# Values times output projection in four 64x64 parts of the array

## The chip, the cores and the metric

The kernel runs on one core of one Trainium2 chip. The metric is the device time of one execution in microseconds (us). A core has five engines that work at the same time, each on its own queue of instructions: TensorE (PE in the profile; PEld is its weight load) multiplies matrices into PSUM, VectorE (DVE) and ScalarE (ACT) copy and compute, GpSimd (POOL) sets constants and starts indirect transfers, and SyncE (SP) starts the other transfers. They wait for one another by semaphores. PSUM has eight banks here; a product writes to one of them and a copy by ACT or DVE takes it out.

## The reference

The reference is one layer of cross attention with a mixture of experts behind it, all in fp32. Queries come from x (4 batches of 1,024 rows of 256), keys and values from a context of 77 rows per batch, with 16 heads of 64:

```python
x = x + xattn(ctx, layernorm(x), fside, fside, ln1_w, ln1_b, ln2_w, ln2_b, Wq, Wkv, Wout)
x = x + ffn(layernorm(x), Wr, Wg, Wu, Wd)      # 9 experts, the two best of each row

# in xattn: queries from x, keys k and values v from the context
qk = einsum('bihd,bjhd->bhij', q, k) * DIM_HEAD ** -0.5
attn = softmax(qk, axis=-1)
out = einsum('bhij,bjhd->bihd', attn, v)       # 16 heads side by side: 1024 columns
return out.reshape(b, -1, INNER) @ Wout
```

What matters here is the last two lines. For a head h, attn_h @ v_h @ Wout_h can be computed as attn_h @ (v_h @ Wout_h). The product v_h @ Wout_h doesn't depend on the queries: it has 77 rows (one for each key) and 256 columns, and is computed once for each batch and head.

## The kernel before, in words

The work has a setup, an attention stage and an expert stage.

The setup loads the context and the weights, normalises the context, and forms two tables for each batch. `g` folds keys with Wq, so that scores are z @ g for a normalised tile z of x. `u` is values times output projection, with nine more columns behind the 256, the router's logits of the same rows (`DE` = 265 columns in all, filled into `wo_sb` by `turn_logits`). `g_half` and `u_half` each hold two batches.

The attention stage takes 32 tiles of 128 rows of x. In tile i the loop issues the scores of tile i in three banks (`scores`: products, then a maximum on DVE), their exponentials on ACT (`exponentials`), then turns the weights of tile i-1 (`weights_turn` on TensorE, `weights_copy` on ACT) and multiplies them with `u` (`values`). `attention_weights` sums and divides on DVE. The expert stage follows with the lists of rows that the router made.

All is issued by hand: `tc.manual_schedule()` leaves each engine's instructions in the order in which the program writes them. An engine works through its queue in this order.

**How u is laid out before.** A key table of 77 rows is split into `JA` = 64 first keys and `JR` = 13 others. Two heads (2n and 2n+1) share one chunk of 128 rows: chunk n of `u` holds the first keys of head 2n in its upper half and those of head 2n+1 in its lower half. That makes `NP` = 8 chunks. The other keys of all 16 heads lie in `NR` = 2 more chunks, padded: a pair of heads has 26 rows in a strip of `W` = 32. So `values` is a sum over `KC` = 10 products.

**How u is computed before.** `context_values(n)` multiplies the normalised context with the value weights of heads 2n and 2n+1; head 2n comes out in partitions 0 to 63 of the bank (64 features), head 2n+1 in 64 to 127. The copies place them block by block into `vbd` (line 589), a table of zeros in which head 2n has the upper left 64x64 block and head 2n+1 the lower right one. `first_keys(b, n)` multiplies this block-diagonal 128x128 table with the 128 rows of Wout of both heads (line 739), and one copy puts the bank into `u`. `other_keys(n)` does it for the other keys of all four batches at once (line 745), and four copies of 26 rows put them into their strips, one for each batch. `evict` gives a copy to DVE for an odd number and to ACT for an even one.

In the order of the queues, five value products come first, with the turn of Wout and the logits between them. The statistics of the first queries follow (`query_stats` to `query_scale`), then eight rounds n: value products while there are any left, four `first_keys`, and one `other_keys` in the middle. In the last rounds the first two tiles of queries and the scores of tile 0 stand between them. The bank of a product comes from `bank_tile`, which uses all eight banks in turn, or from `mm_tile`, which uses five of them once the scores need the other three.

SP's queue holds, in this part, two loads of x, 16 small transfers that put the keys' offsets into the last row of `g` (line 676), and a third load of x.

Of the kernel before, what the change touches and what calls it, by code (L numbers as in the profile page):

```python
# [8 lines left out]
F32 = mybir.dt.float32  # L9
I32 = mybir.dt.int32  # L10
U32 = mybir.dt.uint32
AF = mybir.ActivationFunctionType
ALU = mybir.AluOpType
AX = mybir.AxisListType

P = 128
# [5 lines left out]
def kernel(  # L22
# [18 lines left out]
    nc = tc.nc  # L41

    B, N, D = x.shape
    J = ctx_in.shape[1]
# [16 lines left out]
    NR = 2  # L61
    HR = H // NR
    KC = NP + NR
    W = 32
    NA = KC * P
    DE = D + E
    HB = TB // J
    banks = [(h, min(HB, H - h)) for h in range(0, H, HB)]
    assert banks[-1][1] * J + E <= TB
    assert FT == 64 and DH == 64 and C == 2 and 2 * JR <= W and NP * W == NR * P  # L70
    ATT_SCALE = DH**-0.5


# [48 lines left out]
    def mm_tile(name):  # L122
        return ps_mm.tile([P, TB], F32, tag="mm", name=name)
# [3 lines left out]
    def bank_tile(name):  # L127

        turn_of[0] = (turn_of[0] + 1) % 8
        if turn_of[0] < 5:  # L130
            return mm_tile(name)
        k = turn_of[0] - 5
        return ps_sc.tile([P, TB], F32, tag=f"sc{k}", name=name)

    def evict(k, dst, src):

        if k % 2:
            nc.vector.tensor_copy(dst, src)
        else:
            nc.scalar.copy(dst, src)  # L140
# [65 lines left out]
    def query_stats(g, s):  # L206
        if g not in zstats:
            zstats[g] = stat.tile([P, NS, 6], F32, tag="bnq", name=f"bn_q{g}", bufs=2)
        return nc.vector.bn_stats(zstats[g][:, s, :], xg[g][:, s, :])
# [81 lines left out]
    def attention_weights(i):  # L291

        ex = exs.pop(i)
        sm = stat.tile([P, H], F32, tag="sm", name=f"sm{i}")
        nc.vector.tensor_reduce(sm, ex, AX.X, ALU.add)  # L295
        rs = stat.tile([P, H], F32, tag="rs", name=f"rs{i}")
        nc.vector.reciprocal(rs, sm)
        an = ans[i] = an_of[i % 2]
        nc.vector.tensor_tensor(  # L299
            an[:, : H * JA].rearrange("p (h j) -> p h j", h=H), ex[:, :, 0:JA],  # L300
            rs.unsqueeze(2).to_broadcast([P, H, JA]), ALU.mult,
        )
        nc.vector.tensor_tensor(
            an[:, H * JA :].rearrange("p (n w) -> p n w", w=W)[:, :, : 2 * JR].rearrange(
                "p n (t j) -> p n t j", t=2
            ),
            ex[:, :, JA:J].rearrange("p (n t) j -> p n t j", t=2),
            rs.rearrange("p (n t) -> p n t", t=2).unsqueeze(3).to_broadcast([P, NP, 2, JR]),
            ALU.mult,
        )  # L310

    TURNS = [(k, min(4, KC - k)) for k in range(0, KC, 4)]
# [40 lines left out]
        nc.vector.bn_stats(fstats[g][:, s, :], xg[g][:, s, :])  # L353


    with tc.tile_pool(name="vside", bufs=1) as vside, ExitStack() as kvs:
        kside = kvs.enter_context(tc.tile_pool(name="kside", bufs=1))

        crows = kside.tile([2, D], F32, name="crows")
# [146 lines left out]
        nc.vector.memset(cfold_all, 0.0)  # L506
        cfold = cfold_all[:, :, : 2 * B].rearrange("p n (t b) -> p n t b", t=2)

        TURN = NP - NP // 2
        kT = kside.tile([P, NP, B * J], F32, name="kT")  # L510
        kTs = kside.tile([P, NP, B * J], F32, name="kTs")
# [74 lines left out]
                wc, wr_sb, mean.unsqueeze(1).to_broadcast([P, C, E]), ALU.subtract  # L586
            )

        vbd = vside.tile([P, NP, B, P], F32, name="vbd")
        first = nc.gpsimd.memset(vbd, 0.0)  # L590
        tc.add_manual_dep(
            first.ins, normed.ins.name,
            mybir.DependencyInfo(mybir.DependencyClass.Sync, mybir.DependencyReason.DATA),
            reason="VectorE's work in front of TensorE's first products comes first",
        )
        vrem = vside.tile([P, NP, B, W], F32, name="vrem")
        nc.gpsimd.memset(vrem, 0.0)
        for i in range(2):
            nc.gpsimd.memset(u_half[i][:, :, NP:, :], 0.0)

# [39 lines left out]
        for n in range(NP):  # L640
            if n == 2:
                turn_offsets()
            if n == NP // 2:
                router_weights()
            if n == NP - 2:
                numbers()
            for c in range(C):
                for t in range(2):
                    half = slice(64 * t, 64 * t + 64)
                    pg = bank_tile(f"pgk{n}_{c}_{t}")  # L650
                    nc.tensor.matmul(
                        pg[:, : B * J], wqT[half, n, c * P : (c + 1) * P], kTs[half, n, :],
                        start=True, stop=True,
                    )
                    h = 2 * n + t
                    src = pg[:, : B * J].rearrange("p (b j) -> p b j", b=B)
                    at = slice(h * J, (h + 1) * J)
                    evict(t, g_half[0][:, :, c, at], src[:, :BH])
                    evict(t, g_half[1][:, :, c, at], src[:, BH:])
# [12 lines left out]
        for b in range(B):  # L672
            nc.vector.tensor_copy(g_sb[b][:, :, HJ:], wz)
            for t in range(2):
                for k in range(NP // QT):
                    nc.sync.dma_start(
                        out=g_sb[b][P - 1 : P, C - 1, :HJ].rearrange(
                            "p (k q t j) -> p k q t j", q=QT, t=2, j=J
                        )[:, k, :, t, :],
                        in_=brow.rearrange("(q r) k m -> q r k m", q=QT)[  # L680
                            :, t * B + b, k, b * J : (b + 1) * J
                        ],
                    )
# [25 lines left out]
        def turn_logits():  # L709
            pt = bank_tile("pwlt")  # L710
            for q in range(QB):
                nc.tensor.transpose(
                    pt[:, q * 2 * WC : (q + 1) * 2 * WC], wl[:, q * P : (q + 1) * P],
                    ident[: 2 * WC, : 2 * WC],
                )
            nc.vector.tensor_copy(
                wo_sb[:, :, D:].rearrange("p (i q) e -> p i q e", i=2),
                pt[:, : QB * 2 * WC].rearrange("p (q i e) -> p i q e", q=QB, i=2)[:, :, :, :E],
            )

        def context_values(n):
            pv = bank_tile(f"pv{n}")
            for c in range(C):
                nc.tensor.matmul(
                    pv[:, : B * J], wv_sb[:, c, n * P : (n + 1) * P], cT[:, c, :],
                    start=(c == 0), stop=(c == C - 1),
                )
            for t in range(2):
                half = slice(64 * t, 64 * t + 64)
                src = pv[half, : B * J].rearrange("p (b j) -> p b j", b=B)  # L730
                evict(n, vbd[half, n, :, t * JA : (t + 1) * JA], src[:, :, 0:JA])
                evict(n, vrem[half, n, :, t * JR : (t + 1) * JR], src[:, :, JA:J])

        def key_tile(name, n):
            return bank_tile(name) if n < NP - 1 else mm_tile(name)

        def first_keys(b, n):
            pu = key_tile(f"pu{b}_{n}", n)
            nc.tensor.matmul(pu[:, :DE], vbd[:, n, b, :], wo_sb[:, n, :], start=True, stop=True)
            evict(n + b, u_sb[b][:, n, :], pu[:, :DE])  # L740

        def other_keys(n):

            pu = key_tile(f"pur{n}", n)
            nc.tensor.matmul(
                pu[:, :DE], vrem[:, n].rearrange("p b w -> p (b w)"), wo_sb[:, n, :],
                start=True, stop=True,
            )
            r, q = divmod(n, P // W)
            for b in range(B):  # L750
                evict(
                    n, u_sb[b][q * W : q * W + 2 * JR, NP + r, :],
                    pu[b * W : b * W + 2 * JR, :DE],
                )

        EARLY_V = 5
        QB = TB // P
        for n in range(EARLY_V):
            if n < 2:
                for c in range(C):  # L760
                    turn_wo(n * QB, c)
            elif n == 3:
                wo_logits()
            context_values(n)
        turn_logits()
        for q in range(NS):
            query_stats(0, q)
        query_variance(0)
        query_root(0)
        query_scale(0)  # L770
        for n in range(NP):
            last = n == NP - 1
            if n + EARLY_V < NP:
                context_values(n + EARLY_V)
            if n >= NP - 2:
                query(n - NP + 2)
            for b in range(B):
                if last and b == 2:
                    query_turn(1)
                first_keys(b, n)  # L780
                if b == 1:
                    other_keys(n)
                if last and b < len(banks):
                    scores(0, b)
                    exponentials(0, b)
            if n == 0:

                nc.scalar.activation(junk, eps_t, AF.Exp)
            if n == NP - 2:
                query_turn(0)  # L790
    sent = []

    def after(i, others, reason):
# [587 lines left out]
    for i in range(N_SUB + 1):  # L1381
# [4 lines left out]
        if now_on:  # L1386
# [9 lines left out]
            if i:  # L1396
                scores(i, 2)
        if i:
            weights_turn(i - 1)
            weights_copy(i - 1, 0)  # L1400
            weights_copy(i - 1, 1)
        if now_on and i:
            exponentials(i, 1)
        if 0 < i < N_SUB - 1:
# [149 lines left out]
```

## Time and profile before

| | |
|---|---|
| time, median of 3 runs | 927.01 us (924.75 to 927.33) |
| the profiled execution | 924.82 us |
| its span in the profile | 922.8 us |
| granted TensorE clock, mean | 0.997 |
| TensorE busy | 906.7 us, 98% of the span |
| first keys, line 739 | 64 records, 16.6 us busy |
| other keys, line 745 | 16 records, 4.9 us busy |
| copies of other keys on DVE / on ACT | 6.9 us / 5.9 us busy, 16 each |
| transfers into g, line 676 | 16, issued from 33.93 to 42.99 us |
| first scores of tile 1 begin | 69.75 us |
| first values of tile 0 begin | 76.39 us |

Times in the profile are microseconds from the start of the span. A group line names source line, engine, operation, the tiles written and read, shapes, the count, and after the bar the busy time in us and the mean length of one in ns; behind the second bar stands the idle time before them, with what ended it. An fp32 product shows as two records of MATMUL and two of LDWEIGHTS. `128*64` ahead of a matmul's shape means that 128 rows and 64 columns of the array are in use. The length of a matmul record holds its way through the array, so the pace of a stream is read from the distance of starts. A line of the windows gives a stretch, its length, the busy time of PE, PEld, DVE, ACT and POOL, the granted clock, the busy share of the transfer engines and GB/s.

### The profile page before, as it was taken

The numbers are of one execution on the slowest core, as the hardware profiler recorded it, in microseconds if no ns is written. First come the engines' busy times: TensorE is split into PE (matmuls) and PEld (weight loads), VectorE is DVE, ScalarE is ACT, GpSimd is POOL, SyncE is SP. The second block draws the span as 40 slices with busy tenths as digits, with TensorE's granted clock in tenths as the row PEclk, the third lists the DMA queues.
The fourth block names the chain that finished last, engine by engine and source line by source line (L and its number), as shares of the span: only waits on it lengthen the run. The fifth ranks groups of instructions, "written<-read, shape, count | busy, mean of one in ns | idle before, by whom it ended". The sixth has DMA issues, their size and how long they took to land. (4 is left out here: it accounts for less than half of the span.)

```text
span 922.8 us, 13371 instructions
## 1 busy us (share of the span) xinstructions
PE 906.7 (98%) x4210; PEld 703.5 (76%) x4210; DVE 450.0 (49%) x1330; ACT 341.7 (37%) x1075; POOL 318.2 (34%) x329
## 2 busy tenths in 40 slices
PE   8999999999999999999999999999999999999996
PEld 6676777777777777788888777777777777778885
DVE  5776678888788887763722222222222222222221
ACT  4666575565646566551211122222222222111210
POOL 5000000321504242146454445435435435444432
PEclk9999999999999999999999999999999999999998
DMA  6200010503102710456779779779779777779822
GB/s 216 70 0 1 24 46 25 46 24 46 51 30 59 229 30 24 117 153 172 179 209 299 217 207 307 212 211 313 218 205 310 219 208 227 218 220 312 226 35 23
DMA packets 109125, 137.02 MB, mean 148 GB/s; under 512 B 24247, under 2 KB 79039, under 8 KB 109056
## 3 DMA queue, kind: packets, MB, share of 16 engines
q1 hardware_dynamic: 91498, 118.78, 42.0%
q0 software_dynamic: 17344, 17.26, 10.5%
q8 instruction: 34, 0.56, 0.3%
q14 instruction: 35, 0.29, 0.1%
q10 hardware_dynamic: 214, 0.13, 0.0%
HBM read 119.48 MB, written 18.33 MB: 149 GB/s over the span
## 5 line engine op out<-in xcount | busy, mean ns | idle before, releaser
L1193 PE MATMUL pg<-xT,wgu 128*128 128x256 f32 x1144 | 251.7, 379 | 0.4 <-PEq L1510 0.4
L1193 PEld LDWEIGHTS pg<-xT,wgu 128*128 128x128 f32 x1144 | 215.9, 190 | 29.3 <-issue 0.8
L1267 PE MATMUL po<-wd,hid 128*128 128x256 f32 (+1 forms) x804 | 180.5, 379 | 0.0
L1267 PEld LDWEIGHTS po<-wd,hid 128*128 128x128 f32 (+1 forms) x804 | 147.2, 187 | 21.3 <-issue 0.7
L275 ACT ACTIVATE ex<-psc,mx 128x77 f32<-128x77 f32 x512 | 124.2, 361 | 101.8 <-DVE mx L265 96.7
L1302 POOL DMA_INDIRECT out_dram<-co,ids x63 | 100.7, 1599 | 170.4 <-DVE co L1270 136.4
L918 POOL DMA_INDIRECT list_d<-r_entry,r_pli x64 | 67.2, 1050 | 256.2 <-DVE r_pli L916 124.9
L338 PE MATMUL po<-u,aT 128*128 128x265 f32 x640 | 151.7, 391 | 0.9 <-ACT aT L327 0.8
L261 PE MATMUL psc<-g,zT 128*128 128x462 f32 (+1 forms) x384 | 139.1, 511 | 1.2 <-ACT zT L250 1.2
L338 PEld LDWEIGHTS po<-u,aT 128*128 128x128 f32 x640 | 118.7, 189 | 23.7 <-ACT aT L327 1.9
L1200 DVE TENSOR_TENSOR hid<-pg,sl 128x256 f32<-128x256 f32 x130 | 55.1, 424 | 160.0 <-ACT sl L1199 159.7
L1199 ACT ACTIVATE sl<-pg 128x256 f32<-128x256 f32 x130 | 49.8, 384 | 218.3 <-PE pg L1193 211.9
L261 PEld LDWEIGHTS psc<-g,zT 128*128 128x128 f32 x384 | 72.5, 189 | 59.2 <-issue 49.4
L1270 DVE TENSOR_SCALAR co<-po,ids 128x256 f32<-128x256 f32 x67 | 32.4, 484 | 136.2 <-PE po L1267 136.1
L1151 POOL DMA_INDIRECT yin<-y_d,ids x67 | 70.4, 1051 | 24.7 <-issue 14.7
L265 DVE TENSOR_REDUCE mx<-psc 128x6 f32<-128x462 f32 (+1 forms) x96 | 55.7, 581 | 18.1 <-PE psc L261 15.1
L295 DVE TENSOR_REDUCE sm<-ex 128x16 f32<-128x1232 f32 x32 | 45.9, 1435 | 37.1 <-ACT ex L275 37.1
L327 ACT COPY aT<-pa 128x512 f32<-128x512 f32 (+1 forms) x96 | 49.4, 552 | 26.7 <-PE pa L319 26.7
L319 PEld LDWEIGHTS pa<-ident,an 128*128 128x128 f32 x320 | 36.9, 141 | 7.7 <-PE po L338 1.4
L319 PE MATMUL pa<-ident,an 128*128 128x128 f32 x320 | 40.2, 273 | 1.0 <-DVE an L299 1.0
L299 DVE TENSOR_TENSOR an<-ex,rs 128x1024 f32<-128x1024 f32 x32 | 39.2, 1225 | 1.1
L1255 ACT COPY hid<-ph 128x384 f32<-128x384 f32 x15 | 7.2, 479 | 73.9 <-PE ph L1250 73.9
(312 smaller groups left out, 840.7 us busy)
## 6 DMA issues: line engine op xcount, KB each, us to landing
wgu<-in_L_ffn_Wg_dram SPq DMA_DIRECT2D x41, 704.0 KB
wd<-in_L_ffn_Wd_dram SPq DMA_DIRECT2D x41, 640.0 KB
wgu<-in_L_ffn_Wu_dram SPq DMA_DIRECT2D x41, 512.0 KB
wgu<-in_L_ffn_Wu_dram SPq DMA_DIRECT2D x41, 128.0 KB
x<-in_x_dram SPq DMA_DIRECT2D x8, 512.0 KB
out_dram<-x SPq DMA_DIRECT2D x8, 512.0 KB
y_d<-y SPq DMA_DIRECT2D x8, 512.0 KB
w<-in_L_ffn_Wg_dram SPq DMA_DIRECT2D x5, 704.0 KB
```

What stands on the lines that cost most here:

```text
L261: nc.tensor.matmul(psc[:, :w], zT[:, c, :], g_sb[i // NS // GPB][:, c, h * J : h * J + w], start=(c == 0), stop=(c == C - 1),)
L265: nc.vector.tensor_reduce(nmx[i][:, h : h + n], psc[:, : n * J].rearrange("p (h j) -> p h j", h=n), AX.X, ALU.max, negate=True,)
L275: nc.scalar.activation(exs[i][:, h + q, :], pscs[k][:, q * J : (q + 1) * J], AF.Exp, bias=nmx[i][:, h + q : h + q + 1],)
L319: nc.tensor.transpose(pa[:, q * P : (q + 1) * P], ans[i][:, (k + q) * P : (k + q + 1) * P], ident)
L338: nc.tensor.matmul(po[:, :DE], aT[:, n, :], u_sb[b][:, n, :], start=(n == 0), stop=(n == KC - 1))
L918: i = nc.gpsimd.indirect_dma_start(out=list_d[:, :], out_offset=bass.IndirectOffsetOnAxis(ap=place_i[:, s : s + 1], axis=0), in_=entries[k ...
L1151: return nc.gpsimd.indirect_dma_start(out=dst, out_offset=None, in_=src, in_offset=bass.IndirectOffsetOnAxis(ap=offsets, axis=0), **kw,)
L1193: nc.tensor.matmul(pg[:, g, :], w[:, c, at : at + P], xT[:, c, :], start=(c == 0), stop=(c == C - 1),)
L1199: nc.scalar.activation(sl, pg[:, 0, :], AF.Silu)
L1200: nc.vector.tensor_tensor(hid[:, f, :], pg[:, 1, :], sl, ALU.mult)
L1267: nc.tensor.matmul(po[rows, :D], hid[:, f, at], d[:, f, :], start=(f == 0), stop=(f == NF))
L1302: i = nc.gpsimd.indirect_dma_start(out=out_r, out_offset=bass.IndirectOffsetOnAxis(ap=rows_of(j, h, rows), axis=0), in_=cos[j][:, h, :], i ...
```

## The change

Heads are grouped anew: head pair n and pair n+4 (`N2` = 4) work together. The order of heads in `g`, and with it in the scores and weights, becomes that of `place_of`. The block-diagonal table is gone: `vals` holds the values of both heads of a pair one above the other, 64 features of each and 64 keys, without zeros. `quarters_of` issues four products of 64 rows and 64 columns of the array: with the upper rows for the first head of a pair, with the lower rows for the second, and with the left columns for pair n, the right columns for pair n+4. Each row half writes to a bank of its own, and each column half to its own half of the bank's partitions. A bank then holds the 128 rows of one chunk of `u`, and one copy takes it out; ACT takes the upper rows' bank, DVE the lower rows'.

The other keys go the same way into `urem`, and 32 transfers on SP's queue (`other_keys_placed`) put them from there into their strips of `u`. A strip is now 16 rows for each head (`W` = 16), with 13 in use. The order of the queues is new as well: the statistics of the first queries stand after the fourth value product, all other keys come before the first queries, and first keys fill places between the query turns and scores. Two groups, of batches 2 and 3, are left for tiles 1 and 2, and the pool `vside` is closed after tile 2.

```diff
-    W = 32
+    W = 16
+    N2 = NP // 2
...
+        def place_of(n, t):
+
+            k, q = divmod(n, N2)
+            return (2 * q + t) * 2 + k
...
-        vbd = vside.tile([P, NP, B, P], F32, name="vbd")
-        first = nc.gpsimd.memset(vbd, 0.0)
+        vals = vside.tile([P, NP, B, JA], F32, name="vals")
+        vrem = vside.tile([P, NP, B, W], F32, name="vrem")
+        urem = vside.tile([P, NP, DE], F32, name="urem")
+        first = nc.gpsimd.memset(vrem, 0.0)
...
-                    h = 2 * n + t
+                    h = place_of(n, t)
...
-        def context_values(n):
+        def context_values(k):
+            n = k // 2 + k % 2 * N2
...
-            for t in range(2):
-                half = slice(64 * t, 64 * t + 64)
-                src = pv[half, : B * J].rearrange("p (b j) -> p b j", b=B)
-                evict(n, vbd[half, n, :, t * JA : (t + 1) * JA], src[:, :, 0:JA])
-                evict(n, vrem[half, n, :, t * JR : (t + 1) * JR], src[:, :, JA:J])
...
-        def first_keys(b, n):
-            pu = key_tile(f"pu{b}_{n}", n)
-            nc.tensor.matmul(pu[:, :DE], vbd[:, n, b, :], wo_sb[:, n, :], start=True, stop=True)
-            evict(n + b, u_sb[b][:, n, :], pu[:, :DE])
+            src = pv[:, : B * J].rearrange("p (b j) -> p b j", b=B)
+            evict(k, vals[:, n], src[:, :, 0:JA])
+            evict(k, vrem[:, n, :, :JR], src[:, :, JA:J])
+        def quarters_of(n, name, left, new):
+            pus = [new(f"{name}_{t}") for t in range(2)]
+            for k in range(2):
+                for t, pu in enumerate(pus):
+                    half = slice(64 * t, 64 * t + 64)
+                    nc.tensor.matmul(
+                        pu[64 * k : 64 * k + 64, :DE], left(n + k * N2)[half],
+                        wo_sb[half, n + k * N2, :], start=True, stop=True,
+                    )
+            return pus
+
+        def first_keys(b, n, new):
+            pus = quarters_of(n, f"pu{b}_{n}", lambda m: vals[:, m, b, :], new)
+            for t, pu in enumerate(pus):
+                evict(t, u_sb[b][:, 2 * n + t, :], pu[:, :DE])
...
-            for b in range(B):
-                evict(
-                    n, u_sb[b][q * W : q * W + 2 * JR, NP + r, :],
-                    pu[b * W : b * W + 2 * JR, :DE],
-                )
+            pus = quarters_of(
+                n, f"pur{n}", lambda m: vrem[:, m].rearrange("p b w -> p (b w)"), bank_tile
+            )
+            for t, pu in enumerate(pus):
+                evict(t, urem[:, 2 * n + t, :], pu[:, :DE])
+
+        def other_keys_placed(b):
+            for k in range(2):
+                for q in range(2 * N2 // NR):
+                    at = (2 * q + k) * W
+                    nc.sync.dma_start(
+                        out=u_sb[b][at : at + JR, NP:, :],
+                        in_=urem[64 * k + b * W : 64 * k + b * W + JR].rearrange(
+                            "p (r q) d -> p r q d", r=NR
+                        )[:, :, q, :],
+                    )
...
             context_values(n)
+            if n == 3:
+                for q in range(NS):
+                    query_stats(0, q)
+                query_variance(0)
+                query_root(0)
+                query_scale(0)
         turn_logits()
...
+        context_values(EARLY_V)
+        fill((0, 0), (1, 0), (2, 0), (3, 0), new=bank_tile)
+
+        nc.scalar.activation(junk, eps_t, AF.Exp)
+        context_values(EARLY_V + 1)
+        fill((0, 1), (1, 1), new=bank_tile)
+        context_values(EARLY_V + 2)
+        for n in range(N2):
+            other_keys(n)
+        for b in range(B):
+            other_keys_placed(b)
+        query(0)
+        fill((0, 2), (1, 2))
+        query_turn(0)
+        query(1)
+        fill((0, 3), (1, 3))
+        for k in range(len(banks)):
+            scores(0, k)
+            exponentials(0, k)
+            if k == 0:
+                fill((2, 1), (3, 1))
+                query_turn(1)
+            else:
+                fill((1 + k, 2))
+    left = [(2, 3), (3, 3)]
...
         if i:
+            if i < 3:
+                fill(left[i - 1])
             weights_turn(i - 1)
             weights_copy(i - 1, 0)
             weights_copy(i - 1, 1)
+        if i == 2:
+            vsides.close()
```

## The prediction

> **What bounds the kernel now.** I read the page's busy times first, then busy time by stage, then the groups of the first 110 us with shapes kept apart, then the timeline of TensorE around the change.
>
> The busy times:
>
> ```profile
> PE 906.7 (98%) x4210; PEld 703.5 (76%) x4210; DVE 450.0 (49%) x1330; ACT 341.7 (37%) x1075; POOL 318.2 (34%) x329
> ```
>
> TensorE (PE) works nearly without a pause. A busy PE is a modelled figure, so I check by stage (window, length, then busy time of PE, PEld, DVE, ACT, POOL):
>
> ```profile
> 60.00:65.00 5.00, 4.28 (x18) 2.75 (x17) 2.62 (x8) 2.17 (x7) 0.00 (x0) 1.00 0.00 0
> 75.00:80.00 5.00, 4.32 (x21) 3.33 (x20) 1.83 (x8) 4.98 (x20) 0.00 (x0) 1.00 0.00 0
> 100.00:200.00 100.00, 100.00 (x443) 73.08 (x442) 79.23 (x229) 59.19 (x219) 9.50 (x12) 1.00 0.21 38
> 330.00:920.00 590.00, 582.11 (x2738) 467.85 (x2736) 196.23 (x562) 143.56 (x377) 253.75 (x218) 1.00 0.70 198
> ```
>
> From 100 us on PE is full at a granted clock of 1.00. Nothing there waits for a point in time: weights start when buffers come free. So what the setup gains by the third tile of queries should reach the end undiminished. Between 60 and 80 us PE has gaps; there other engines have a say.
>
> The groups of the first 110 us (matmul count is in records, two to each fp32 product; after the bar busy us, mean ns):
>
> ```profile
> L739 PE MATMUL pu<-wo_sb,vbd 128*128 128x265 f32 x64 | 16.6, 387 | 0.0
> L651 PE MATMUL pgk<-kTs,wqT 64*128 64x308 f32 x64 | 9.2, 430 | 0.0
> L745 PE MATMUL pur<-wo_sb,vrem 128*128 128x265 f32 x16 | 4.9, 387 | 0.0
> L663 PE MATMUL pb<-kT,cfold 128*32 128x308 f32 x16 | 1.2, 428 | 0.0
> L663 PEld LDWEIGHTS pb<-kT,cfold 128*32 128x32 f32 x16 | 0.4, 108 | 0.7 <-ACT g L140 0.4
> L138 DVE COPY u<-pur 26x265 f32<-26x265 f32 x16 | 6.9, 431 | 1.8 <-PE pur L745 1.6
> ```
>
> And TensorE's timeline (start, length):
>
> ```profile
> 35.72 2.24 PE L724 MATMUL pv<-cT,wv_sb 128*128 128x308 f32 x8
> 37.89 1.91 PE L703 MATMUL pwl<-woT,wc 128*32 128x512 f32 x8
> 39.73 2.34 PE L724 MATMUL pv<-cT,wv_sb 128*128 128x308 f32 x8
> ...
> 51.41 1.95 PE L739 MATMUL pu<-wo_sb,vbd 128*128 128x265 f32 x8
> 53.20 0.61 PE L745 MATMUL pur<-wo_sb,vrem 128*128 128x265 f32 x2
> ...
> 61.47 0.61 PE L739 MATMUL pu<-wo_sb,vbd 128*128 128x265 f32 x2
> 62.80 1.82 PE L261 MATMUL psc<-g,zT 128*128 128x462 f32 x4 [0.72 <-ACT zT L250]
> ...
> 68.64 0.61 PE L739 MATMUL pu<-wo_sb,vbd 128*128 128x265 f32 x2
> 69.75 1.43 PE L261 MATMUL psc<-g,zT 128*128 128x462 f32 x3 [0.50 <-ACT zT L250]
> ```
>
> Eight records from 51.41 to 53.20: 0.224 us a record, so **0.447 us per 265-column product**. After 61.47 and 68.64 the array is idle from 61.92 to 62.80 and from 69.09 to 69.75, 1.5 us together.
>
> **The change, part by part.**
>
> *Fewer passes.* Removed are 32 products with vbd and 8 with vrem, 40 x 0.447 = 17.9 us. Added are 20 groups of four 64x64 products (16 for first keys, 4 for the others). If the four run side by side, a group takes 0.447 us, together 8.9 us: **saved 8.9 us**. No row shows a 64x64 part. Near rows: two row halves to two banks (L651) run 32 products of 308 columns in 9.2 us, 0.29 each where one alone streams 0.224 x 308/265 = 0.26 per record, 0.52 per product: side by side. Four column groups (L663): 8 products in 1.2 us, where one after another would be 4.2. Upper bound: only one axis overlaps, 0.894 per group, nothing saved. I take 0.447, because both axes are shown and the parts share neither a row half with a column half nor a bank.
> A rule speaks against it: the Trainium skill ("TensorE: Matmul & The Clock Gate", Part 3, What overlaps and what doesn't) says a weight load overlaps running products only where the row group differs; parts with the same rows would then queue their loads. The L663 rows disagree: all 128 rows, four column groups, 16 loads of 108 ns (1.7 us in sum) inside 0.4 us. By the rule, about four loads of 0.137 us (the mean of the trace's 64-column loads) stand open per group, 20 x 0.55 = 11 us more, about 931; by the row nothing. I go by the row.
>
> *Switching the array's layout.* The Trainium skill ("TensorEngine Tiling (Array Packing)", Key Properties) says a change of tiling drains TensorE. The trace prices it: pv should end at 35.72 + 8 x 0.26 = 37.80, pwl starts 0.09 later; pwl should take 4 x 0.432 = 1.73 and is followed after 1.84, 0.11 over; the next pv takes 2.34 where the former took 2.24, 0.10 over. So **about 0.32 us in and out**. The new order has nine islands of parts between full products (n=0; n=1; other keys with n=2; n=3; one after the first scores, one after the second, one after the third; one in each of tiles 1 and 2): 2.9 us, seven of them (2.2) ahead of tile 1's scores. The page gives no price, so by the rule alone this stands at nothing or more; the sum takes the trace's.
>
> *Copies.* Other keys: 32 copies of 26 rows (6.9 us busy on DVE, 5.9 on ACT) become 8 of 128 rows, and 32 half-height copies of values become 16. Both engines then need 0.28 to 0.35 us per group (their spacing in runs of u copies) against PE's 0.447: hidden. It would cost if PE were not the slower of the three.
>
> *Statistics of the first queries moved ahead of wo_sb's logit columns.* On DVE the chain from bn_q through ACT's root to the reciprocal took 2.3 us (42.65 to 44.98). Now it begins after the fourth value copy, at 41.6, and wo_sb's copy behind it ends near 44.1; PE could start the first group at 43.6. **0.5 us lost**. Behind the same root on ACT waits one value copy, not needed before n=2. In return z is ready early.
>
> *Transfers.* 32 transfers of 13 partitions x 2 rows of 1,060 bytes go on SP's queue, behind the 16 of g and ahead of the third load of x. The 16 of g were issued in 9.06 us, 0.57 each, and the last landed 1.3 us after its issue. Other keys are copied out by about 52.0 in my timetable; batch 0's eight transfers land by 52.0 + 8 x 0.57 + 1.3 = 57.9. The first product with chunk 8 comes near 72.5. **Hidden, 14 us to spare.** The third x is issued near 70 instead of 43; its first reader stood at 105.84. The last batches are read from tile 16 on. GpSimd loses a memset of 3.5 us that nobody waited for.
>
> *The order at the end.* Groups now stand between query turns and scores, so the 1.5 us of idle time is filled. Two groups are left for tiles 1 and 2.
>
> *The sum.* Up to tile 1's first scores 22 product slots go (40 less 18): 9.8 us; less seven islands 2.2; plus 1.5 idle; less 0.5: they start **8.6 us earlier**, at 61.15 instead of 69.75. Then PE isn't alone: the first values wait for max, exponentials, sum, weights, turn and copy. DVE gets one u copy (0.35) in front of the second x's statistics and the sum, and ACT one (0.3) in front of the aT copy; the earlier start of the scores does not speed this chain. By lengths from the trace: third maximum at 60.6, u copy to 61.5, four bn_q to 62.8, sum and weights to 65.8, next maximum to 66.6, six exponentials to 67.9, u copy to 68.2, first aT copy, first values at 68.9 instead of 76.39: **7.5 earlier**, and tile 1's group lies in that wait. In tile 2 PE sets the pace again: its group costs 0.45 + 0.32 = 0.75. **Net 6.8 us.**
>
> The profiled execution took 924.82 (span 922.8); by it 918.0. The three runs have the median 927.01, so I predict **920.2**. Changes within 0.3% (2.8 us) can't be told from none.
>
> **Rivals.**
> 1. *Parts overlap only in pairs.* Row halves side by side, column halves with the same rows one after another, as the rule on loads would have it. A group takes 0.894: 20 x 0.447 = 8.9 us dearer than forecast, 929.1, slower than before. The break-even is 0.447 + 6.8/20 = 0.79 us per group. For it: no 64x64 row in the trace. Against: both axes are shown singly. Chance 0.10.
> 2. *The transfers take the wait's place.* Values of tile 0 stall once batch 0's eight exceed (72.5 - 52.0 - 1.3)/8 = 2.4 us each, four times the 0.57 seen; at 3 us they cost 4.8 and give 925. For it: 26 descriptors each instead of 4. Against: 512 KB loads of x are issued in 0.41. Chance 0.04.
> 3. *Side by side, but the gain is eaten* by dearer switches (0.55 each) and bank waits in the new order: 2 to 3 us more, 922.5 to 924.5, and in part no change. Chance 0.14.
> 4. *The chain at tile 1 is shorter than laid out and switches hide in waits*: all 8.6, 918.4. Within the forecast case.
>
> **How the numbers follow.** Forecast with rival 4: 0.70, its own range 917 to 923, faster. Rival 3: 0.14, of which 0.10 faster and 0.04 the same. Rival 2: 0.04, half the same, half slower. Rival 1: 0.10, slower. Slower in ways I don't see: 0.02. Faster 0.70 + 0.10 = 0.80; same 0.04 + 0.02 = 0.06; slower 0.10 + 0.02 + 0.02 = 0.14. Range 916.5 to 925.5: all of the forecast case and of rival 3's upper end, without rival 1.
>
> **What would show it.** Right: groups of eight records of 64x64 spaced 0.447 us; tile 1's first scores near 61 and first values near 69; steady tiles still 10.1 us apart (before, scores at 91.00 and 101.08); the wait at the first chunk 8 absent. Wrong: groups 0.9 us apart; PE idle behind a transfer of u; more than 0.5 us between an island and its neighbours; or a tile spacing above 10.1 later, since weights of other keys now lie 16 to a head.

## The result, and the profile after

| | before | after |
|---|---|---|
| time, median of six runs each | 925.07 us (924.75 to 927.33) | 918.03 us (917.28 to 919.82) |
| the profiled execution | 924.82 us | 918.41 us |
| its span | 922.8 us | 916.6 us |

The ratio is 0.9921, with a 95% interval of 0.9905 to 0.9936: 7.0 us less, where 6.8 were forecast. Of the 2.2 us between the forecast of 920.2 and the result, 1.9 come from the base it was taken from: three runs of the kernel before had the median 927.01, six have 925.07, and 925.07 less 6.8 is 918.3. By the interval the saving lies between 5.9 and 8.8 us, so that 7.0 and 6.8 agree to 0.2 is closer than these times can show; the profiles below give the finer measure.

The busy times of the changed kernel, from the page:

```profile
PE 900.5 (98%) x4290; PEld 693.3 (76%) x4290; DVE 442.1 (48%) x1310; ACT 334.5 (36%) x1055; POOL 314.9 (34%) x328
```

TensorE is busy for 6.2 us less, and the span is 6.2 us shorter; its share stays 98%. Its idle time is 16.1 us in both, so the time follows its work. By stage (window, length, busy time of PE, PEld, DVE, ACT, POOL, granted clock, share of the transfer engines, GB/s):

```profile
68.00:73.00 5.00, 3.98 (x18) 3.22 (x19) 1.90 (x9) 4.98 (x21) 0.00 (x0) 1.00 0.16 34
73.00:81.00 8.00, 8.00 (x41) 5.14 (x40) 5.81 (x13) 5.93 (x16) 0.00 (x0) 1.00 0.16 32
100.00:200.00 100.00, 100.00 (x440) 73.08 (x438) 78.47 (x227) 62.62 (x227) 14.41 (x16) 1.00 0.20 38
```

Of the gaps between 60 and 80 us one is left, in front of tile 0's first values (68 to 73 us); from 73 us on TensorE is full, and the attention stage is as full as it was. The groups of the first 110 us, with shapes kept apart:

```profile
L746 PE MATMUL pu<-wo_sb,vals 64*64 64x265 f32 x128 | 9.2, 396 | 0.3 <-DVE wo_sb L722 0.3
L746 PEld LDWEIGHTS pu<-wo_sb,vals 64*64 64x64 f32 x128 | 4.1, 132 | 5.2 <-issue 2.4 <-DVE wo_sb L722 0.8 <-PE psc L263 0.7
L746 PE MATMUL pur<-wo_sb,vrem 64*64 64x265 f32 x32 | 2.0, 389 | 0.0
```

The first keys have twice the records of before and take 9.2 us instead of 16.6; the other keys take 2.0 instead of 4.9. One record is as long as before (396 ns, 387 then), so the parts lie beside each other in time. The weight loads say the same: 128 of 132 ns would be 16.9 us one after another, and all of them fit into 4.1 us.

TensorE's timeline, in the same rows as before the change:

```profile
42.47 0.46 PE L718 MATMUL pwlt<-ident,wl 64*128 64x64 f32 x4
42.86 1.30 PE L731 MATMUL pv<-cT,wv_sb 128*128 128x308 f32 x4
44.51 2.02 PE L746 MATMUL pu<-wo_sb,vals 64*64 64x265 f32 x32 [0.34 <-DVE wo_sb L722]
46.45 1.30 PE L731 MATMUL pv<-cT,wv_sb 128*128 128x308 f32 x4
...
59.11 0.68 PE L746 MATMUL pu<-wo_sb,vals 64*64 64x265 f32 x8
59.72 1.33 PE L263 MATMUL psc<-g,zT 128*128 128x317 f32 x4
60.98 0.68 PE L746 MATMUL pu<-wo_sb,vals 64*64 64x265 f32 x8
61.59 4.43 PE L263 MATMUL psc<-g,zT 128*128 128x462 f32 x12
65.96 0.68 PE L746 MATMUL pu<-wo_sb,vals 64*64 64x265 f32 x8
66.57 1.31 PE L317 MATMUL pa<-ident,an 128*128 128x128 f32 x10
68.97 0.44 PE L250 MATMUL pz<-ident,z 128*128 128x128 f32 x2 [1.10 <-ACT u L142]
69.46 4.75 PE L336 MATMUL po<-u,aT 128*128 128x265 f32 x20
74.05 4.33 PE L263 MATMUL psc<-g,zT 128*128 128x462 f32 x12
...
84.83 4.33 PE L263 MATMUL psc<-g,zT 128*128 128x462 f32 x12
```

Four groups take from 44.51 to 46.45, 1.94 us: 4 x 0.447 = 1.79 and 0.15 for the change of layout. One group between two score banks makes the way from 59.11 to 60.98, 1.87 us; less 0.447 and less four records of 317 columns (4 x 0.268 = 1.07) there remain 0.35 us for going into parts and out again. Tile 1's scores begin at 61.59 (69.75 before), tile 0's values at 69.46 (76.39), and tile 3's scores at 84.83 (91.00). The values run through all ten chunks without a stop. The last two starts in the kernel before:

```profile
76.39 4.75 PE L338 MATMUL po<-u,aT 128*128 128x265 f32 x20 [0.61 <-ACT aT L327]
91.00 4.33 PE L261 MATMUL psc<-g,zT 128*128 128x462 f32 x12
```

### The profile page after: what moved, and what is told of

The parts are those of the page before. It is cut to its first block, busy times and chain, and to the rows that moved or that the text cites. A ratio compares the mean times of both kernels' runs of the same rounds, so it can differ in the third digit from the quotient of the medians.

```text
span 916.6 us, 13532 instructions
## 1 busy us (share of the span) xinstructions
PE 900.5 (98%) x4290; PEld 693.3 (76%) x4290; DVE 442.1 (48%) x1310; ACT 334.5 (36%) x1055; POOL 314.9 (34%) x328
## 3 DMA queue, kind: packets, MB, share of 16 engines
q0 software_dynamic: 17344, 17.26, 10.6%
```

## The experiments

A profiled execution starts its part of the change not always at the same point (41.8 to 45.4 us; what is known of the reason is in the last section). So all are measured from the turn of the logits (line 718, or the line that answers it), the last step that all kernels reach in the same way. The **stretch** is the time from there to tile 3's first scores, after which the tiles are alike. The columns up to the stretch come from one profiled execution of each kernel, in us from that turn. Times are medians of 4 to 15 runs; each ratio is taken against the kernel before on the same chip.

| kernel | tile 1's scores | first values | tile 2's scores | stretch | time | ratio, 95% |
|---|---|---|---|---|---|---|
| before | 27.74 | 34.38 | 38.97 | 49.00 | 925.07 | |
| after | 19.12 | 26.99 | 31.57 | 42.36 | 918.03 | 0.9921 (0.9905 to 0.9936) |
| e1_pairs | 28.04 | 35.90 | 40.49 | 51.72 | 927.05 | 1.0025 (1.0011 to 1.0039) |
| e5_rows | 19.14 | 27.01 | 31.59 | 42.38 | 918.38 | 0.9926 (0.9900 to 0.9952) |
| e2_front | 19.41 | 27.28 | 31.87 | 41.90 | 918.12 | 0.9927 (0.9909 to 0.9945) |
| e3_stats | 18.83 | 26.69 | 31.28 | 42.07 | 917.54 | 0.9924 (0.9909 to 0.9938) |
| e7_last | 19.12 | 26.99 | 41.20 | 52.71 | 928.64 | 1.0048 (1.0033 to 1.0063) |
| e4_xlate | 19.12 | 26.99 | 31.57 | 42.36 | 918.60 | 0.9929 (0.9915 to 0.9942) |
| e6_bn | 19.11 | 26.19 | 30.78 | 41.56 | 917.87 | 0.9927 (0.9912 to 0.9941) |
| e9_all | 19.10 | 26.98 | 31.56 | 41.60 | 916.90 | 0.9911 (0.9897 to 0.9925) |
| e10_best | 18.83 | 25.16 | 29.65 | 40.44 | 915.49 | 0.9895 (0.9876 to 0.9914) |
| after_again | 19.11 | 26.98 | 31.57 | 42.35 | 917.29 | 0.9920 (0.9901 to 0.9939) |

The stretch of the changed kernel is the same in two profiles of it on two occasions (42.36, 42.35), while the medians of its runs differ by 0.7 us. Effects under 1 us are therefore read from the stretch.

**e1_pairs: everything of the change but the four parts at once.** The values go into two tables padded with zeros, one for each half of the partitions, and the products use all 128 rows and 64 columns. Order, grouping of heads, the 32 transfers and the number of TensorE's instructions stay. The copies of values come in halves again, as in the kernel before, and the first loads of x start late again, at 32.9 us (e4_xlate shows that their place does not change the stretch).

```diff
-        vals = vside.tile([P, NP, B, JA], F32, name="vals")
+        vals = [vside.tile([P, NP, B, JA], F32, name=f"vals{t}") for t in range(2)]
...
-                    half = slice(64 * t, 64 * t + 64)
                     nc.tensor.matmul(
-                        pu[64 * k : 64 * k + 64, :DE], left(n + k * N2)[half],
-                        wo_sb[half, n + k * N2, :], start=True, stop=True,
+                        pu[64 * k : 64 * k + 64, :DE], left(n + k * N2, t),
+                        wo_sb[:, n + k * N2, :], start=True, stop=True,
                     )
```

> The changed kernel with its order, but each part multiplies 128 rows instead of 64: the values of each head stand in a table of their own whose other half is zero, so only the two column halves can run side by side. If the gain comes from four parts at a time, a group takes 0.894 us instead of 0.447, tile 3's scores move from 84.8 to about 92.9 (18 groups x 0.447 = 8.0, and 0.45 for the group in tile 2, less 0.4 where the loads of x come later again), and the time is near 926, no faster than before. If the new order and the larger copies made the gain, it stays at 918 to 920.

The groups of the first 110 us of this kernel, with shapes kept apart:

```profile
L749 PE MATMUL pu<-wo_sb,vals 128*64 128x265 f32 x128 | 16.5, 395 | 1.2 <-DVE wo_sb L724 1.2
```

And a row of TensorE's timeline:

```profile
44.68 3.85 PE L749 MATMUL pu<-wo_sb,vals 128*64 128x265 f32 x32 [1.17 <-DVE wo_sb L724]
```

The same number of records takes 16.5 us where the changed kernel takes 9.2: a group costs 0.894, two parts at a time. The stretch is 9.36 us longer than that of the changed kernel. Twenty groups dearer by 0.447 make 8.94; the first waits 1.17 us for `wo_sb` instead of 0.34, because the copies in halves stand ahead of it on DVE (0.83 more); and tile 1's longer group takes 0.45 from a wait that stands there in any case. Together 9.32; the expectation had left out the 0.83. Against the kernel before, this one is 2.7 us longer in the stretch and slower in time. Of the 2.7, 0.8 are its own, from the halved copies; the new order, the islands and the transfers together bring nothing and cost the other 1.9. **The four parts at once are the whole gain.** It is also rival 1's case made real: 1.9 us above the kernel before on the same chip (927.05 against 925.15), where that rival stood 2.1 above its base.

**e5_rows: parts with the same rows next to each other.** The two loops of `quarters_of` change places, so that products with the same rows and different columns follow each other directly.

```diff
-            for k in range(2):
-                for t, pu in enumerate(pus):
+            for t, pu in enumerate(pus):
+                for k in range(2):
```

> The changed kernel with the four parts of a group in the other order: both column halves of the upper rows, then both of the lower rows. If weight loads of parts with the same rows wait for one another, this order has two such neighbours where the other has one, and groups get wider than 0.447 us, time 920 or more. If all four run side by side whatever their order, the pace is the same and the time 918.

The stretch is 42.38. If weights of the same rows had to wait for running products, this order would have met that at every second part; in the changed kernel's order no two neighbours have the same rows (the expectation counts one such pair). Here it makes no difference in which of the two orders the parts are issued. The rule of the Trainium skill that the prediction argued against ("TensorE: Matmul & The Clock Gate", Part 3) shows no effect in either order.

**e2_front: all first keys in one run.** The groups that stand between turns and scores, and those in tiles 1 and 2, move ahead of the first query's turn. Nine islands become three.

```diff
-        fill((0, 2), (1, 2))
+        fill((0, 2), (1, 2), (2, 1), (3, 1), (2, 2), (3, 2), (0, 3), (1, 3), (2, 3), (3, 3),
+             new=bank_tile)
         query_turn(0)
         query(1)
-        fill((0, 3), (1, 3))
+        query_turn(1)
...
-            if k == 0:
-                fill((2, 1), (3, 1))
-                query_turn(1)
-            else:
-                fill((1 + k, 2))
-    left = [(2, 3), (3, 3)]
...
-            if i < 3:
-                fill(left[i - 1])
```

> The changed kernel with all first-key groups in one stretch ahead of the query turns and scores: three islands of parts instead of nine. If switching costs 0.35 us a pair and filled idle time is worth 1.5 us, the two cancel up to tile 1's scores (61.6 in both), tile 2 saves its group's 0.75, tile 3's scores come at 84.1 and the time is 917.3. If switches are cheap and the filled idle time is what counts, tile 1's scores come at 63 and the time is 919.5 or more.

TensorE's timeline of this kernel:

```profile
52.35 4.64 PE L746 MATMUL pu<-wo_sb,vals 64*64 64x265 f32 x80
56.93 0.44 PE L250 MATMUL pz<-ident,z 128*128 128x128 f32 x2
58.00 0.41 PE L250 MATMUL pz<-ident,z 128*128 128x128 f32 x2 [0.63 <-DVE z L241]
58.24 8.50 PE L263 MATMUL psc<-g,zT 128*128 128x462 f32 x24
```

Ahead of tile 1's scores four islands less give 4 x 0.35 = 1.4 us, two groups more cost 0.89, so the scores should come 0.5 earlier. They come 0.29 later: 0.8 us of waiting is back, in front of the second turn, where the line shows 0.63 from the modelled end of the first. In tile 2 the group taken out gives 0.76 us (scores 10.03 us apart instead of 10.79). The balance is 0.46 us in the stretch, where 0.75 was expected, and none that the times can show. The six islands saved are worth 2.1 us, and 1.6 of them go into waits.

**e3_stats: the first queries' statistics back behind the logits.**

```diff
-            if n == 3:
-                for q in range(NS):
-                    query_stats(0, q)
-                query_variance(0)
-                query_root(0)
-                query_scale(0)
         turn_logits()
+        for q in range(NS):
+            query_stats(0, q)
+        query_variance(0)
+        query_root(0)
+        query_scale(0)
```

> The changed kernel with the statistics of the first queries back behind the turn of the logits, as the kernel before has them. The prediction charged 0.5 us for having them ahead. If that is so, the first group starts 0.4 earlier and the stretch from the turn of the logits to tile 3's scores shrinks from 42.4 us to about 41.9. If the copies behind the root on ACT and behind the statistics on DVE hold the banks back instead, the stretch stays at 42.4 or grows. The time itself is 917.5 or 918, not to be told apart.

The wait of 0.34 us for `wo_sb` is gone and the first groups follow the value product at once. The stretch is 0.29 us shorter, where 0.5 was expected. So this move of the change costs 0.3 us.

**e7_last: batch 0's other keys placed last.** The transfers are issued in the opposite order of batches; no work is added.

```diff
-        for b in range(B):
+        for b in reversed(range(B)):
             other_keys_placed(b)
```

> The changed kernel with the transfers of the other keys issued for batch 3 first and batch 0 last. SP issues one each 0.87 us from 52.1, so batch 0 lands at 82 instead of 61. If the transfers are hidden only by their place in the queue, tile 0's values wait at chunk 8 from 73.0 to about 82, and the time is 926 to 928. If transfers of this kind never matter, it stays at 918.

TensorE's timeline of this kernel at the first values:

```profile
68.83 3.85 PE L336 MATMUL po<-u,aT 128*128 128x265 f32 x16
81.13 2.11 PE L336 MATMUL po<-u,aT 128*128 128x265 f32 x4 [8.46 <-DMA u<-urem]
83.03 5.05 PE L263 MATMUL psc<-g,zT 128*128 128x462 f32 x12
```

Its windows (the granted clock is the number behind the five engines):

```profile
81.00:84.00 3.00, 2.87 (x6) 2.04 (x7) 0.50 (x2) 0.00 (x0) 0.00 (x0) 0.50 0.36 141
84.00:90.00 6.00, 6.00 (x33) 3.40 (x31) 2.93 (x7) 2.48 (x9) 0.00 (x0) 0.96 0.00 0
```

And SP's timeline of it:

```profile
51.40 27.92 SPq L769 DMA_DIRECT2D u<-urem  x32
```

Chunk 8 waits from 72.4 (16 records of 0.224 behind 68.83) to 81.13, 8.7 us (the line's 8.46 counts from the modelled end of the records), for a transfer that is issued as one of the last eight, up to 79.3. Then TensorE works at half its clock: the four records of chunks 8 and 9 take 1.90 us instead of 0.9, the next scores 4.98 instead of 4.26. That is 8.7 + 1.0 + 0.7 = 10.4, and the stretch is 10.35 longer. The time goes up by 10.6 and past the kernel before. Rival 2's mechanism is real, and **the order of the batches is what hides it**.

**e4_xlate: the loads of x behind the setup's weights.** In the changed kernel the first two loads of x had moved from 33 us to 4 us, beside the loads of the weights; the prediction did not see this. Here they wait for the last product of the key offsets.

```diff
+        tc.add_manual_dep(
+            load_x(0).ins, pb_last.ins.name,
+            mybir.DependencyInfo(mybir.DependencyClass.Sync, mybir.DependencyReason.DATA),
+            reason="the weights come first",
+        )
```

> The changed kernel, but the first loads of x wait for the last product that reads the setup's tables, as they did before for their memory; in the changed kernel they start at 4 us beside the weights. If that costs the setup, the turn of the logits comes at 41.8 to 42.0 instead of the 41.8 to 44.0 seen so far, and the time is about 0.5 to 1 us shorter, near 917.3. If the spread at the start has another cause, the time stays at 918.0 and the turn still moves about.

The stretch does not change, and the logits' turn comes at 44.37, later than in any profile of the changed kernel (42.47, 41.77). The early loads are not what moves that point. The windows of this kernel show what did here:

```profile
12.00:16.00 4.00, 4.00 (x11) 2.65 (x10) 0.96 (x2) 0.83 (x2) 1.41 (x23) 0.57 1.04 411
```

Those of the changed kernel:

```profile
12.00:16.00 4.00, 4.00 (x17) 2.96 (x16) 1.50 (x4) 1.66 (x4) 1.75 (x23) 1.00 1.04 378
```

At a clock of 0.57 the same 4 us hold 11 matmul records instead of 17. The first 20 records with `wk_sb` begin 0.21 us later than in the changed kernel and take 1.69 us more, together the 1.90 us between 42.47 and 44.37. The six times of this kernel lie in two clusters, 917.3 to 917.6 and 919.6 to 920.2; the profiled execution belongs to the upper one.

**e6_bn: what sets tile 0's first values.** Four statistics of the second x stood in front of the sum on DVE. In tile 1 they move behind the maxima.

```diff
-            if g + 1 < NG:
+            if g + 1 < NG and i:
                 for k in range(NS):
...
+            if i == 1:
+                for k in range(NS):
+                    query_stats(1, k)
```

> The changed kernel with the statistics of the second load of x moved on DVE from ahead of tile 0's sum to behind tile 1's maxima. If the first values wait for the chain of DVE and ACT as the prediction laid it out, the sum starts 0.8 us earlier, as soon as the exponentials end, the first values too, and the stretch from the turn of the logits to tile 3's scores is 41.6 instead of 42.4. If PE sets the pace there, it stays at 42.4.

DVE's timeline of the changed kernel:

```profile
61.76 0.43 DVE L140 COPY u<-pu 128x265 f32<-128x265 f32 x1 [0.18 <-PE pu L746]
62.11 1.39 DVE L211 BATCH_NORM_STATS2 bn_q<-x 128x6 f32<-128x256 f32 x4
63.42 1.42 DVE L297 TENSOR_REDUCE sm<-ex 128x16 f32<-128x1232 f32 x1
```

That of e6_bn:

```profile
61.21 0.43 DVE L140 COPY u<-pu 128x265 f32<-128x265 f32 x1 [0.18 <-PE pu L746]
62.06 1.44 DVE L297 TENSOR_REDUCE sm<-ex 128x16 f32<-128x1232 f32 x1 [0.42 <-ACT ex L277]
```

From the copy to the sum it took 1.66 us and takes 0.85. First values and stretch come 0.80 us earlier, though TensorE's work is the same: DVE's chain sets this point, as the prediction had it. The expectation of 41.6 is met (41.56).

**e9_all: the front run with the moved statistics.** e2_front, e4_xlate and e6_bn together, and the second query's work ahead of the groups, so that its turn need not wait.

```diff
-        fill((0, 2), (1, 2))
-        query_turn(0)
         query(1)
-        fill((0, 3), (1, 3))
+        fill((0, 2), (1, 2), (2, 1), (3, 1), (2, 2), (3, 2), (0, 3), (1, 3), (2, 3), (3, 3),
+             new=bank_tile)
+        query_turn(0)
+        query_turn(1)
```

> The changed kernel with three edits: all first-key groups in one stretch with both query tiles prepared ahead of them, the loads of x late, the second x's statistics behind tile 1's maxima. If the parts of the setup are what the runs so far say, the stretch from the turn of the logits to tile 3's scores is 40.6 to 41.0 (41.9 with the groups in one stretch, 0.5 less for the query turn that waited for its tile, 0.5 to 0.8 less for the statistics), and the time is 916.0 to 916.5, 1.5 to 2 us under the changed kernel. If idle time just moves from one place to another, it stays at 918.

The stretch is 41.60 us, and the time 916.90; both miss the expectation (at most 41.0, and 916.5). TensorE's timeline of this kernel:

```profile
58.59 8.60 PE L263 MATMUL psc<-g,zT 128*128 128x462 f32 x24 [0.24 <-ACT zT L252]
68.00 1.31 PE L317 MATMUL pa<-ident,an 128*128 128x128 f32 x10 [0.81 <-DVE an L301]
69.70 0.44 PE L250 MATMUL pz<-ident,z 128*128 128x128 f32 x2 [0.39 <-DVE z L241]
70.74 4.75 PE L336 MATMUL po<-u,aT 128*128 128x265 f32 x20 [0.60 <-ACT aT L325]
```

With nothing between the scores they come one after another, and the chain of maximum, exponentials, sum and turn behind them is what TensorE waits for: 0.81, 0.39 and 0.60 us. The wait at the second turn that e2_front had is smaller, and it is back further down. First values stand where they stood.

**e10_best: the islands kept, the chain shortened.** e3_stats and e6_bn, and in tile 1 the copies of tile 0's turned weights go on ACT ahead of tile 1's first exponentials, with the left-over group behind them.

```diff
                 scores(i, 0)
+            if i > 1:
                 exponentials(i, 0)
...
-            if i < 3:
-                fill(left[i - 1])
+            if i == 2:
+                fill(left[1])
             weights_turn(i - 1)
...
+            if i == 1:
+                weights_copy(0, 2)
+                fill(left[0])
+                exponentials(1, 0)
...
-        if i:
+        if i > 1:
             weights_copy(i - 1, 2)
```

> The changed kernel with four edits of order: the first queries' statistics behind the logits' turn; the second x's statistics behind tile 1's maxima; in tile 1 the copies of tile 0's turned weights on ACT ahead of tile 1's exponentials; and tile 1's left group behind them. If the first values wait for ACT's queue, they come 0.9 earlier than with the second edit alone, and the stretch from the turn of the logits to tile 3's scores is 40.4 us (41.56 with the second edit, less 0.3 for the first, less 0.9), 1.9 under the changed kernel; the time is about 916.2. If the later exponentials hold up tile 2 in turn, it stays at 41.3.

> The changed kernel once more, beside the last version on the same chip: 918.0, the stretch from the turn of the logits to tile 3's scores 42.36 us.

The stretch is 40.44 us as expected, 1.9 shorter than the changed kernel's: 0.3 by e3_stats, 0.8 by e6_bn, so about 0.8 is left for the new order in tile 1 (copies first, group behind them), if the effects add. That order was not run alone. Tile 0's first product with values follows at once, without a wait, in TensorE's timeline of e10_best:

```profile
68.48 1.26 PE L317 MATMUL pa<-ident,an 128*128 128x128 f32 x10
69.67 0.68 PE L746 MATMUL pu<-wo_sb,vals 64*64 64x265 f32 x8
70.28 0.44 PE L250 MATMUL pz<-ident,z 128*128 128x128 f32 x2
70.55 4.65 PE L336 MATMUL po<-u,aT 128*128 128x265 f32 x20
```

Its median is 915.49 us (914.31 to 918.37), 1.8 us under the changed kernel on the same chip (917.29). The two intervals against the kernel before overlap, so the times alone do not prove the step between the two; the stretch gives it the same size. No other kernel run has a lower median.

## Why the prediction was right

**Pace of a group: right.** 0.447 us was taken. Ten groups in e2_front last 4.64 us and four in the changed kernel 2.02, which makes 0.44 for each further group, and e1_pairs gives back 8.94 us of the gain when only two parts run at once. The rows L651 and L663 were the right neighbours to read, and the rule on loads would have put the time on the wrong side. One reason was put too widely: the two column halves of a row half do share a bank, each with its own half of the partitions, and the pace is 0.447 all the same.

**Switching: right.** 0.32 us was read from the rows around pwl (its three parts add up to 0.30); an island costs 0.35, far from the 0.55 of rival 3. That is nine times 0.35, 3.2 us in all, but e2_front gets only 0.5 back without six of them.

**First scores and first values: right.** They were put at 61.15 and 68.9 with the logits' turn where it was before, at 42.00. It came at 42.47 in this profile; the measured 61.59 and 69.46, less 0.47, are 61.12 and 68.99. The 0.47 lies in the setup: the first product with `wk_sb` begins at 11.07 instead of 10.60, when the weights are there (10.36 in after_again). That the values would be held by DVE and ACT and not by TensorE, so that 8.6 us become 7.5, is what e6_bn shows: 0.80 us off DVE's chain is 0.80 us off the stretch. Rival 4, with the whole 8.6, does not occur: the scores come 8.6 us earlier, the values 7.4.

**Tile 2's group: right.** 0.75 was worked out, 0.76 measured (10.79 between tile 2's and tile 3's scores, 10.03 without it).

**Carried to the end: right.** From tile 3's scores to the first product of the experts it takes 303.13 us before (91.00 to 394.1) and 303.16 after (84.83 to 388.0). The stretch is 6.64 us shorter and the logits' turn 0.47 later, which leaves the 6.2 us between the spans.

**Statistics: mis-sized.** They were priced at 0.5 us; e3_stats measures 0.3. The wait for `wo_sb` is 0.34, and without it the four groups that follow take 0.1 longer.

**Idle time: right.** The 1.5 us between 60 and 70 us were counted as filled by the groups. With the measured sizes the sum up to tile 1's scores closes: 22 x 0.447 = 9.8, less 7 x 0.35 = 2.45, plus 1.5, less 0.3 for the statistics is 8.6, and 27.74 less 19.12 is 8.6. That the forecast sum gave 8.6 too is in part luck: the islands cost 0.25 more than was put down for them and the statistics 0.2 less. The 0.8 us that e2_front brings back are no measure of this term, as its queue differs from the one before the change: both turns stand next to each other.

**Transfers: mis-sized, with no effect.** 0.57 us each was taken from those of `g`. SP's timeline of the changed kernel:

```profile
33.41 8.81 SPq L682 DMA_DIRECT2D g<-brow  x16
52.04 28.15 SPq L769 DMA_DIRECT2D u<-urem  x32
80.23 0.52 SPq L204 DMA_DIRECT2D x<-in_x_dram  x1
```

28.15 / 32 = 0.88 us each, half as much again. Batch 0's eight are issued by 59.1, and with the prediction's 1.3 us to landing they are there at 60.4, not 57.9; chunk 8 reads them at 73.0, so some 12.6 us were to spare by this estimate, and not 14. The third x is issued at 80, not 70, still ahead of its reader. That the slack was real and the order needed, e7_last shows.

**Not seen: the early loads of x**, which by e4_xlate do nothing to the stretch, and the clock in the setup.

## What to carry to other kernels

Four products of 64 rows and 64 columns cost here what one full product costs (fp32, 265 columns), with a bank for each row half and half of the bank's partitions for each column half; other layouts were not run. A block-diagonal table is then worth taking apart even at the price of 0.35 us for each island of parts. Before merging such islands, look at what they cover: between scores and weights they stood in waits for other engines, and merging them gave back 0.5 us of 2. And once a stage has no gap on the busiest engine but at one place, shorten the chain that ends at that place (0.8 us for statistics that stood in the way, about 0.8 more, by difference, where the order in tile 1 was changed); at the same time put first on a transfer queue what is read first.

## What the runs showed of the hardware that was not expected

TensorE's clock fell to half after pauses and made them dearer. After the 8.7 us in e7_last it was 0.50 for 3 us and 0.96 over the next 6, 1.7 us lost; by these two rows half clock lasted about 3.4 us (2.87 us of work at 0.50, and 0.5 us more in the next 6). The Trainium skill ("TensorE: Matmul & The Clock Gate", Part 1) describes this: half rate after an idle window of about 3.4 us, and full rate after as long a busy one. In the setup it came after shorter pauses too, and not each time. TensorE waited there for the first loads. Waits of 2.17 us in the changed kernel and of 2.78 in e2_front left the clock at 1.00; waits of 2.67 in e5_rows, 2.72 in e4_xlate and 3.52 in e10_best were followed by a lower one, and so was one of only 1.35 in e9_all (TensorE's timeline and two windows):

```profile
10.67 6.59 PE L520 MATMUL pk<-cT,wk_sb 128*128 128x308 f32 x18 [1.35 <-DMA wk_sb<-in_L_xattn_Wkv_dram]
10.00:12.00 2.00, 1.33 (x3) 0.96 (x4) 0.09 (x1) 0.00 (x0) 2.00 (x3) 0.73 1.04 416
12.00:14.00 2.00, 2.00 (x5) 1.33 (x4) 0.48 (x1) 0.41 (x1) 2.00 (x23) 0.50 1.01 383
```

The page lets the window run free of the kernel, which would make it a matter of chance; no run here tells what decided it. In the four kernels whose clock fell the logits' turn came at 43.8 to 45.4 us, in the others at 41.8 to 43.0.

The time SP needs to issue a transfer went with its shape: 0.55 us for one into `g` with 4 rows of 308 bytes, 0.88 for one into `u` with 26 rows of 1,060 bytes.
